# Cross-attention in an fp32 decoder layer: scores in two row halves, values in four column quarters, weights divided on GpSimd

## The chip, the cores and the metric

The kernel runs on one core of one Trainium2 chip. The metric is the device time of one execution in microseconds (us); less is better. A core has five engines that matter here: PE (TensorE, matrix products), DVE (VectorE), ACT (ScalarE), POOL (GpSimd) and SP, which here only issues DMAs. Each engine works off its own queue strictly in the order in which the program was written, and waits on semaphores for the others.

## The reference, cut to what matters

One pre-norm decoder layer, all in fp32, for x of 4 batches x 1024 rows x 256 columns:

```python
x = x + self_attention(layernorm(x))                     # 16 heads of 64, 4 key-value heads
x = x + cross_attention(layernorm(x), ctx, mask)         # 16 heads of 16, 64 keys per batch
x = x + feed_forward(layernorm(x))                       # routed, with small splines per row

def cross_attention(query, context, mask):               # the part that is changed
    q  = query @ Wq + bq
    kv = context @ Wkv + bkv                             # split into k and v, 16 heads each
    scores = einsum("bhid,bhjd->bhij", q, k) * 256**-0.5
    scores = where(mask[:, None, None, :], -inf, scores)
    out = einsum("bhij,bhjd->bhid", softmax(scores), v)
    return out @ Wout + bout
```

With a mask that hides every key of a batch the softmax is not a number; the inputs drawn hide none.

## The kernel before, in words

The rows of a batch lie in tiles of 128 (eight a batch, 32 in all). Self-attention is the body: for each tile, four "duos" of four heads each (`duo`, L551). A duo makes scores in two halves of the PE's rows (L577, 64 x 512), takes their maxima on DVE (L591), the exponentials on ACT (L597), turns the weights either on DVE with DMAs (L606, L633) or on PE (L616), multiplies with the values in two column halves (L656), and spreads the inverse sums over the partitions by a small product (`spread`, L682).

**Cross-attention** (`cross_attention`, L780) takes two tiles at a time (TX = 2). After the layernorm (`layernorm`, L390, whose rsqrt runs on POOL, L406 and L407), its transposes and the query projection (L797), each of the two tiles of 128 queries goes through these steps:

- `scores` (L818): for each half c of the columns, one matmul of the 128 query columns with `kblk`, a block matrix of 128 x (8 heads x 64 keys). `block_k` (L744) makes it once a batch, by multiplying the keys with the 0/1 pattern `own` (L303), so that a head's 16 rows meet only its own 64 columns. The rest of the block is zero.
- `masked` (L821): DVE adds the mask's row out of PSUM into `sc`, 128 x (16 heads x 64 keys); `largest` (L833): the maximum by head on DVE; `less` (L836): POOL subtracts it; `exponential` (L839): ACT.
- `flips` (L850, group L854) and `evict` (L856): eight transposes on PE, copied to `pT` by ACT (L857).
- `values` (L868): eight matmuls, each with 128 x 128 of the weights stationary and 34 columns of `vblk` streaming: two heads of 16 value columns and, for each, one column of ones (`keep`, L313 and `block_v`, L764), which yields the sum of the weights. Masked keys have zeros there.
- `divide` (L872): DVE takes the reciprocal of the sums out of PSUM (L873) and multiplies (L874); `flip_o` (L886, group L888): two transposes on PE; `evict_o` (L890): ACT; `project_o` (L898); `evict_p` (L902) on DVE; `residual` (L905) on POOL.

**The order of the work** is made by a planner (`Flow`, L78). `add` hands it a task with an engine, a cost in us, a key (a due time), the tasks that it needs and the buffers that it takes; `order` (L120) places, one at a time, the task that can start first by these costs and lags (0.2 to 0.3 us between engines), urgent ones first (the maxima and exponentials of self-attention), and never with a key more than `AHEAD` = 16 over the front. The code is emitted in this order; on the chip each engine keeps it, even where the costs were wrong. Buffers have places by tag (L226): the scores of cross-attention (`xsc`), `xpT` and `xoT` have one each, so the second tile's scores wait until the first one's weights are turned. Three PSUM buffers of one bank (`p1`, L240) serve everything but self-attention's scores and outputs.

**The feed-forward block** (`feed_forward`, L991) follows for every four tiles (the last four in two blocks of two), mostly in many small DVE steps, with its last steps on POOL (`finish`, L1144).

Of the kernel before, what the change touches and what calls it, by code (L numbers as in the profile page):

```python
# [10 lines left out]
F32 = mybir.dt.float32  # L11
U8 = mybir.dt.uint8
AF = mybir.ActivationFunctionType
ALU = mybir.AluOpType
# [13 lines left out]
XC = 8  # L28
# [164 lines left out]
def decoder(  # L193
# [35 lines left out]
            xmx=2, xpT=1, xrs=2, xo=1, xoT=1, xf=1, fxT=1, hT=1, sc=1, comp=2, cal=1, fm=4, hot=1, hotT=1,  # L229
            par=1, hh=1, mag=2,  # L230
        ),
        {"p1", "ln", "res", "rb", "rsum", "nmax"},
# [67 lines left out]
    for i in range(NCL):  # L300
        nc.gpsimd.memset(falling[:, i : i + 1], float(NCL - i))

    own = const.tile([P, XC], F32, name="own")  # L303
    nc.gpsimd.memset(own, 1.0)
    nc.gpsimd.affine_select(
        out=own, in_=own, compare_op=ALU.is_ge, fill=0.0, base=0, pattern=[[-XD, XC]], channel_multiplier=1
    )
    nc.gpsimd.affine_select(
        out=own, in_=own, compare_op=ALU.is_ge, fill=0.0, base=XD - 1, pattern=[[XD, XC]], channel_multiplier=-1
    )  # L310
# [5 lines left out]
    add("DVE", 0.2, 2, lambda: nc.vector.tensor_scalar(keep, kmask8, -1.0, 1.0, ALU.mult, ALU.add), [kmask_], [keep_])  # L316
# [40 lines left out]
    quants = buf("xo", work, 2, DC, NTILES, name="quants")  # L357
# [193 lines left out]
    def duo(b, d):  # L551
# [6 lines left out]
        ss = sums[b, qt]  # L558
        prob = Buf("prob", lambda: work.tile([P, 4 * S], F32, tag="prob", name=f"prob_{b}_{d}"))
# [86 lines left out]
        for part in range(2):  # L646
            def values(part=part):
# [20 lines left out]
                holds=[heads[b, qt]],  # L668
# [52 lines left out]
    def context(b, at):  # L721


        kblk = kblks[b] = buf("kblk", big, DC, XC, SK, name=f"kblk_{b}")
        vblk = vblks[b] = buf("vblk", big, XH // 2, 2, XD + 1, name=f"vblk_{b}")
# [18 lines left out]
        def block_k(c):  # L744
            nc.vector.tensor_tensor(
                kblk.t[:, c],
                kt.t[:, c, :].unsqueeze(1).to_broadcast([P, XC, SK]),
                own.unsqueeze(2).to_broadcast([P, XC, SK]),
                ALU.mult,
            )  # L750
# [13 lines left out]
        def block_v():  # L764
            vt4 = vt.t.rearrange("p (g t d) -> p g t d", t=2, d=XD)
            for half in range(2):
                r = slice(half * SK, (half + 1) * SK)
                nc.vector.tensor_scalar(vblk.t[r, :, half, :XD], vt4[r, :, half, :], keep[r, b : b + 1], None, ALU.mult)
                nc.vector.tensor_copy(vblk.t[r, :, half, XD], keep[r, b : b + 1].to_broadcast([SK, XH // 2]))
# [10 lines left out]
    def cross_attention(b, t0, at):  # L780
# [31 lines left out]
        for k in range(TX):  # L812
            now = at + 2 + 3 * k
            sc = buf("xsc", work, XH, SK, name=f"xsc_{name}_{k}")
            for c in range(DC):
                ps = psum1(f"xs_{name}_{k}_{c}")

                def scores(c=c, ps=ps, k=k):  # L818
                    mm(ps.t, lhsT=qT.t[:, c, k * P : (k + 1) * P], rhs=kblk.t[:, c], start=True, stop=True)  # L819

                def masked(c=c, ps=ps, sc=sc):  # L821
                    nc.vector.tensor_tensor(  # L822
                        sc.t[:, XC * c : XC * (c + 1), :],
                        ps.t.rearrange("p (h k) -> p h k", k=SK),
                        mneg[:, b, :].unsqueeze(1).to_broadcast([P, XC, SK]),
                        ALU.add,
                    )

                add("PE", 0.9, now, scores, [qT, kblk], [ps], holds=[sc])
                add("DVE", 0.68, now, masked, [ps, mneg_], [sc])  # L830
# [14 lines left out]
            add("ACT", 1.07, now, exponential, [sc], [sc])  # L845
            pT = buf("xpT", work, XH // 2, P, name=f"xpT_{name}_{k}")
            for g in range(2):
# [12 lines left out]
                add("ACT", 0.6, now + 2, evict, [pt], [pT])  # L860
            av = psum1(f"xav_{name}_{k}")
            rs = buf("xrs", small, XH, name=f"xrs_{name}_{k}")
            o = buf("xo", work, D, name=f"xo_{name}_{k}")

            def rows_of(av=av):
                return av.t[:, : XH * (XD + 1)].rearrange("p (h d) -> p h d", h=XH)

            def values(av=av, pT=pT, rows_of=rows_of):  # L868
                for g in range(XH // 2):
                    mm(rows_of(av)[:, 2 * g : 2 * g + 2, :], lhsT=pT.t[:, g, :], rhs=vblk.t[:, g], start=True, stop=True)  # L870

            def divide(av=av, rs=rs, o=o, rows_of=rows_of):  # L872
                nc.vector.reciprocal(rs.t, rows_of(av)[:, :, XD])  # L873
                nc.vector.tensor_tensor(  # L874
                    o.t.rearrange("p (h d) -> p h d", d=XD),
                    rows_of(av)[:, :, :XD],
                    rs.t.unsqueeze(2).to_broadcast([P, XH, XD]),
                    ALU.mult,
                )

            add("PE", 2.1, now + 3, values, [pT, vblk], [av], holds=[rs, o])
            add("DVE", 0.7, now + 3, divide, [av], [rs, o])
            pt = psum1(f"pxo_{name}_{k}")
            oT = buf("xoT", work, DC, P, name=f"xoT_{name}_{k}")

            def flip_o(pt=pt, o=o):  # L886
                for c in range(DC):
                    flip(pt.t[:, c * P : (c + 1) * P], o.t[:, c * P : (c + 1) * P], ident)  # L888

            def evict_o(pt=pt, oT=oT):  # L890
                nc.scalar.copy(oT.t.rearrange("p c q -> p (c q)"), pt.t[:, :D])

            add("PE", 0.3, now + 4, flip_o, [o], [pt], holds=[oT])
# [382 lines left out]
```

## Time and profile before

| | |
|---|---|
| median of three runs | 1993.22 us (1990.15 to 1993.29) |
| the profiled execution | 1997.92 us, of which 1996.2 from the first to the last instruction (span) |
| mean granted PE clock | 0.965 |
| busy: PE, DVE, ACT, POOL | 1864.4, 1538.9, 964.2, 267.2 us |
| HBM traffic | 13.37 MB read, 4.19 MB written |

How to read it: a group is a source line, an engine and an operation, with "out<-in" by the names in the program. After it come the shapes, the count, the busy time in us and the mean length of one in ns, and behind the second bar the idle time of the engine just before these instructions and what ended it. A PE row counts records: an fp32 matmul is two of them, a transpose one. PEld rows are weight loads, which overlap the matmuls. "128*64" is the part of the array in use, rows x columns. Records of neighbours overlap in the profile, since the end of a matmul is modelled; the start of the next group tells more than the length. The chain that ended last is followed back from the last instruction, at each step to what released it.

### The profile page before, as it was taken

What the parts mean: (1) busy time and instruction counts of PE and PEld (TensorE: products, weight loads), DVE (VectorE), ACT (ScalarE), POOL (GpSimd) and SP (SyncE); (2) the same over time, 40 slices, a digit from 0 to 9 for tenths busy, and PEclk for the clock granted to TensorE, in tenths of its full rate; (3) what the DMA queues carried; (4) which work ended last, traced back from release to release, by engine and by line L of the source; (5) the groups of instructions that cost most, each with busy time, mean ns of one, the idle gap of its engine ahead of it and who ended that gap; (6) DMA issues with size and microseconds to landing.
All of it is one profiled execution on the core that took longest, in us unless ns stands there. A gap on an engine that the chain in (4) does not pass through costs nothing.

```text
span 1996.2 us, 30371 instructions
## 1 busy us (share of the span) xinstructions
PE 1864.4 (93%) x11204; PEld 1114.0 (56%) x11204; DVE 1538.9 (77%) x2447; ACT 964.2 (48%) x1730; POOL 267.2 (13%) x422
## 2 busy tenths in 40 slices
PE   7899999999999999989999999989999999997973
PEld 4455555655566555556556555655556655564542
DVE  4767787897788878787778878887778877778853
ACT  2545455555445555545445545454545554553431
POOL 1000101030010301121000311103001030010322
PEclk9899999999999999989999999998999999998975
DMA  3555554454455455545454456535455435545510
GB/s 132 127 127 137 127 132 109 105 121 108 104 127 117 94 122 123 123 110 127 96 116 107 95 128 137 122 75 127 96 122 127 101 91 127 113 100 127 119 24 5
DMA packets 87859, 220.92 MB, mean 111 GB/s; under 512 B 26336, under 2 KB 36896, under 8 KB 87712
## 3 DMA queue, kind: packets, MB, share of 16 engines
q1 hardware_dynamic: 85440, 212.42, 47.3%
q0 software_dynamic: 1168, 4.19, 0.6%
q8 instruction: 89, 1.46, 0.3%
q10 hardware_dynamic: 1104, 2.37, 0.3%
q14 instruction: 58, 0.48, 0.1%
HBM read 13.37 MB, written 4.19 MB: 9 GB/s over the span
## 4 chain that ended last, share of the span: by engine, by line
PE 81%; DVE 12%; ACT 3%; DMA 1%; issue 1%; SPq 1%; POOL 1%; POOLq 0%; ACTq 0%; DVEq 0%
PE s L577 25%; PE av L656 22%; DVE nmax L591 6%; PE pq L530 5%; PE po L709 5%; PE ptp L616 5%; PE rb L682 2%; PE xav L870 2%; PE xs L819 2%; PE pxq L797 2%; ACT prob L597 2%; PE pv L502 2%; DVE prob L606 1%; PE pk L479 1%; PE pg L1097 1%; PE pxp L900 1%
## 5 line engine op out<-in xcount | busy, mean ns | idle before, releaser
L597 ACT ACTIVATE prob<-s,nmax 128x1024 f32<-128x1024 f32 x512 | 569.2, 1115 | 581.0 <-DVE nmax L591 571.3
L591 DVE TENSOR_REDUCE nmax<-s 128x1 f32<-128x1024 f32 x512 | 602.1, 1217 | 211.4 <-PE s L577 210.6
L577 PE MATMUL s<-kT,qT 64*128 64x512 f32 x2048 | 545.4, 621 | 9.3 <-ACT prob L597 9.0
L656 PE MATMUL av<-probT,vn 128*64 128x256 f32 x4096 | 479.6, 385 | 2.7 <-DMA probT<-prob 2.5
L606 DVE STREAM_TRANSPOSE prob<-prob 128x1024 f32<-128x1024 f32 x384 | 460.3, 1225 | 20.5 <-ACT prob L597 15.3
L656 PEld LDWEIGHTS av<-probT,vn 128*64 128x64 f32 x4096 | 284.0, 137 | 204.1 <-issue 70.5
L577 PEld LDWEIGHTS s<-kT,qT 64*128 64x128 f32 x2048 | 196.2, 187 | 216.6 <-issue 170.2
L620 ACT COPY probT<-ptp 128x512 f32<-128x512 f32 x256 | 138.9, 594 | 127.7 <-PE ptp L616 127.7
L616 PE MATMUL ptp<-ident,prob 128*128 128x128 f32 x1024 | 147.6, 281 | 20.5 <-ACT probT L620 5.0
L616 PEld LDWEIGHTS ptp<-ident,prob 128*128 128x128 f32 x1024 | 109.9, 141 | 76.4 <-issue 31.2
L530 PE MATMUL pq<-ln_T,wq 128*128 128x256 f32 x512 | 132.2, 407 | 4.2 <-DMA wq<-in_w_qT 3.7
L837 POOL TENSOR_TENSOR xsc<-xsc,xmx 128x1024 f32<-128x1024 f32 x32 | 61.0, 1908 | 497.0 <-DVE xmx L834 252.6
L709 PE MATMUL po<-wo,heads 128*128 128x256 f32 x512 | 121.1, 386 | 1.9 <-DVE xsc L822 1.8
L530 PEld LDWEIGHTS pq<-ln_T,wq 128*128 128x128 f32 x512 | 99.2, 202 | 32.8 <-issue 15.0
L709 PEld LDWEIGHTS po<-wo,heads 128*128 128x128 f32 x512 | 94.2, 190 | 34.5 <-issue 15.9
L715 POOL TENSOR_TENSOR x<-x,res 128x256 f32<-128x256 f32 x32 | 23.3, 728 | 620.9 <-DVE res L712 516.6
L597 ACT ACTIVATION_READ_ACCUMULATOR prob<-s,nmax 128x1 f32 x512 | 100.8, 197 | 0.0
L541 ACT ACTIVATE qT<-pq,bqs,qscale 128x256 f32<-128x256 f32 x128 | 65.3, 563 | 49.6 <-PE pq L530 49.2
L695 DVE TENSOR_TENSOR heads<-av,rb 128x256 f32<-128x256 f32 x128 | 53.0, 414 | 46.7 <-PE av L656 45.6
L682 PEld LDWEIGHTS rb<-ident,rsum 128*64 128x64 f32 x1024 | 54.6, 136 | 59.0 <-issue 45.4
L682 PE MATMUL rb<-ident,rsum 128*64 128x128 f32 x1024 | 83.3, 284 | 4.2 <-DVE xres L903 4.2
L819 PE MATMUL xs<-kblk,xq 128*128 128x512 f32 x128 | 67.9, 653 | 1.7 <-ACT xq L806 1.7
(162 smaller groups left out, 1526.9 us busy)
## 6 DMA issues: line engine op xcount, KB each, us to landing
probT<-prob SPq DMA_DIRECT2D x1536, 128.0 KB, 2.3
ln_n<-in_x SPq DMA_DIRECT2D x16, 256.0 KB, 3.1
x<-in_x SPq DMA_DIRECT2D x8, 512.0 KB, 4.2
out<-ln_n POOLq DMA_DIRECT2D x7, 512.0 KB, 3.5
wo<-in_w_oT SPq DMA_DIRECT2D x1, 1024.0 KB, 13.3
wq<-in_w_qT ACTq DMA_DIRECT2D x1, 1024.0 KB, 9.6
rowv<-in_rows ACTq DMA_DIRECT2D x1, 774.0 KB, 11.7
xwkv<-in_xw_kv SPq DMA_DIRECT2D x1, 512.0 KB, 13.1
```

The lines of the kernel that those rows point to most:

```text
L530: mm(pq.t[:, 2 * P * k : 2 * P * (k + 1)], lhsT=wq[:, dc, (c + k) * P : (c + k + 1) * P], rhs=xTs[b].t[:, dc, 2 * P * w : 2 * P * (w + 1)] ...
L541: nc.scalar.activation(qTs[b, w, c + k].t, pq.t[:, 2 * P * k : 2 * P * (k + 1)], AF.Identity, bias=bqs[:, c + k : c + k + 1], scale=qscale,)
L577: mm(ps[z].t[:, 512 * g : 512 * (g + 1)], lhsT=q.t[r, (qt % 2) * P : (qt % 2 + 1) * P], rhs=kT.t[r, 512 * g : 512 * (g + 1)], start=True, ...
L591: nc.vector.tensor_reduce(nmax.t, ps[z].t, AX.X, ALU.max, negate=True)
L597: nc.scalar.activation(weights(prob.t, z, i), src, AF.Exp, bias=nmax.t, accum_out=ss.t[:, k : k + 1])
L606: nc.vector.transpose(t, t)
L616: flip(pt.t[:, j * P : (j + 1) * P], weights(prob.t, z, i)[:, kc * P : (kc + 1) * P], ident)
L620: nc.scalar.copy(to[:, z, 4 * g : 4 * g + 4, i, :], pt.t.rearrange("p (c q) -> p c q", q=P))
L656: mm(av.t[r, :], lhsT=vns[b, kc // 2].t[:, kc % 2, j * HD : (j + 1) * HD], rhs=rhs, start=(kc == 0), stop=(kc == NT - 1),)
L682: mm(pr.t[r, i * P : (i + 1) * P], lhsT=rs.t[:, k : k + 1].to_broadcast([P, HD]), rhs=ident, start=True, stop=True,)
L709: mm(po.t[:, :D], lhsT=hT.t[:, c, :], rhs=wo[:, c, :], start=(c == 0), stop=(c == QC - 1))
L819: mm(ps.t, lhsT=qT.t[:, c, k * P : (k + 1) * P], rhs=kblk.t[:, c], start=True, stop=True)
```

## The change

Five things change, all in cross-attention.

1. **Scores.** `kblk` and `own` shrink from 8 heads side by side to 4. One task makes all scores of a tile: per half c two matmuls of 64 rows with 256 columns, one in each row half of the array, each row half into its own PSUM buffer. The mask is then added in four steps of 256 elements and not two of 512.
2. **Sums.** The columns of ones leave `vblk`. POOL adds the two halves of the keys (512 results) and their halves (256), DVE adds the remaining 16 per head and takes the reciprocal, and POOL multiplies the weights, ahead of their transposes.
3. **Values.** `vblk` becomes the stationary operand, 128 x 32 (two heads), and `pT` streams with 128 columns. Four such products stand beside each other in column quarters of the array, and the result is the turned output. `flip_o` and its PSUM buffer go; ACT copies `av` to `oT`.
4. **Mask.** Since the sums now take in no `keep`, `keep` is multiplied once by 1/(1 - smallest mask entry of the batch): one where a key is left, infinite where none is. This takes five small DVE steps at the start.
5. **Planner.** The costs handed to it change with the tasks; `pT` is followed in two parts; the tag `xo` is replaced by `xhalf`, and `xrs` has one place, not two.

Nothing of self-attention or the feed-forward block changes, nor any DMA. The diff, without the lines that only rename a tag or a variable:

```diff
@@ -226,10 +226,10 @@
         dict(
             s=2, p1=3, o=1, x=3, xn1=2, xT=1, kT0=1, kT1=1, vn=4, qT=12, prob=2, probT=2, sums=3, nmax=4,
             heads=1, rb=1, rsum=2, res=1, ln=2, xxT=1, xqT=1, kblk=1, vblk=1, xkt=1, xvt=1, xsc=1,
-            xmx=2, xpT=1, xrs=2, xo=1, xoT=1, xf=1, fxT=1, hT=1, sc=1, comp=2, cal=1, fm=4, hot=1, hotT=1,
+            xmx=2, xpT=1, xrs=1, xhalf=1, xoT=1, xf=1, fxT=1, hT=1, sc=1, comp=2, cal=1, fm=4, hot=1, hotT=1,
             par=1, hh=1, mag=2,
         ),
-        {"p1", "ln", "res", "rb", "rsum", "nmax"},
+        {"p1", "ln", "res", "rsum", "nmax", "rb"},
     )
     add = flow.add
 
@@ -300,20 +300,33 @@
     for i in range(NCL):
         nc.gpsimd.memset(falling[:, i : i + 1], float(NCL - i))
 
-    own = const.tile([P, XC], F32, name="own")
+    own = const.tile([P, XC // 2], F32, name="own")
     nc.gpsimd.memset(own, 1.0)
-    nc.gpsimd.affine_select(
-        out=own, in_=own, compare_op=ALU.is_ge, fill=0.0, base=0, pattern=[[-XD, XC]], channel_multiplier=1
-    )
-    nc.gpsimd.affine_select(
-        out=own, in_=own, compare_op=ALU.is_ge, fill=0.0, base=XD - 1, pattern=[[XD, XC]], channel_multiplier=-1
-    )
+    for r in (slice(0, HD), slice(HD, P)):
+        nc.gpsimd.affine_select(
+            out=own[r], in_=own[r], compare_op=ALU.is_ge, fill=0.0, base=0, pattern=[[-XD, XC // 2]],
+            channel_multiplier=1,
+        )
+        nc.gpsimd.affine_select(
+            out=own[r], in_=own[r], compare_op=ALU.is_ge, fill=0.0, base=XD - 1, pattern=[[XD, XC // 2]],
+            channel_multiplier=-1,
+        )
 
 
     keep = const.tile([P, B], F32, name="keep")
     mneg = const.tile([P, B, SK], F32, name="mneg")
     keep_, mneg_ = Buf(), Buf()
-    add("DVE", 0.2, 2, lambda: nc.vector.tensor_scalar(keep, kmask8, -1.0, 1.0, ALU.mult, ALU.add), [kmask_], [keep_])
+    none = const.tile([P, B], F32, name="none")
+
+    def kept():
+
+        nc.vector.tensor_scalar(keep, kmask8, -1.0, 1.0, ALU.mult, ALU.add)
+        nc.vector.tensor_reduce(none, rmask8.rearrange("p (b k) -> p b k", b=B), AX.X, ALU.min)
+        nc.vector.tensor_scalar(none, none, -1.0, 1.0, ALU.mult, ALU.add)
+        nc.vector.reciprocal(none, none)
+        nc.vector.tensor_tensor(keep, keep, none, ALU.mult)
+
+    add("DVE", 1.2, 2, kept, [kmask_, rmask_], [keep_])
     add(
         "DVE", 0.4, 2,
         lambda: nc.vector.tensor_scalar(mneg.rearrange("p b k -> p (b k)"), rmask8, MASKED, None, ALU.mult),
@@ -720,9 +734,8 @@
 
     def context(b, at):
 
-
-        kblk = kblks[b] = buf("kblk", big, DC, XC, SK, name=f"kblk_{b}")
-        vblk = vblks[b] = buf("vblk", big, XH // 2, 2, XD + 1, name=f"vblk_{b}")
+        kblk = kblks[b] = buf("kblk", big, DC, XC // 2, SK, name=f"kblk_{b}")
+        vblk = vblks[b] = buf("vblk", big, XH // 2, 2, XD, name=f"vblk_{b}")
         kt, vt = buf("xkt", small, DC, SK, name=f"xkt_{b}"), buf("xvt", small, D, name=f"xvt_{b}")
         pk, pv = psum1(f"pxk_{b}"), psum1(f"pxv_{b}")
 
@@ -744,8 +757,8 @@
         def block_k(c):
             nc.vector.tensor_tensor(
                 kblk.t[:, c],
-                kt.t[:, c, :].unsqueeze(1).to_broadcast([P, XC, SK]),
-                own.unsqueeze(2).to_broadcast([P, XC, SK]),
+                kt.t[:, c, :].unsqueeze(1).to_broadcast([P, XC // 2, SK]),
+                own.unsqueeze(2).to_broadcast([P, XC // 2, SK]),
                 ALU.mult,
             )
 
@@ -765,8 +778,7 @@
             vt4 = vt.t.rearrange("p (g t d) -> p g t d", t=2, d=XD)
             for half in range(2):
                 r = slice(half * SK, (half + 1) * SK)
-                nc.vector.tensor_scalar(vblk.t[r, :, half, :XD], vt4[r, :, half, :], keep[r, b : b + 1], None, ALU.mult)
-                nc.vector.tensor_copy(vblk.t[r, :, half, XD], keep[r, b : b + 1].to_broadcast([SK, XH // 2]))
+                nc.vector.tensor_scalar(vblk.t[r, :, half, :], vt4[r, :, half, :], keep[r, b : b + 1], None, ALU.mult)
 
         add("PE", 0.9, at, project_k, [xwkv_, cT_], [pk], holds=[kt, kblk, vblk])
         add("DVE", 0.5, at, evict_k, [pk, colv_], [kt])
@@ -812,22 +824,31 @@
         for k in range(TX):
             now = at + 2 + 3 * k
             sc = buf("xsc", work, XH, SK, name=f"xsc_{name}_{k}")
-            for c in range(DC):
-                ps = psum1(f"xs_{name}_{k}_{c}")
-
-                def scores(c=c, ps=ps, k=k):
-                    mm(ps.t, lhsT=qT.t[:, c, k * P : (k + 1) * P], rhs=kblk.t[:, c], start=True, stop=True)
-
-                def masked(c=c, ps=ps, sc=sc):
-                    nc.vector.tensor_tensor(
-                        sc.t[:, XC * c : XC * (c + 1), :],
-                        ps.t.rearrange("p (h k) -> p h k", k=SK),
-                        mneg[:, b, :].unsqueeze(1).to_broadcast([P, XC, SK]),
-                        ALU.add,
-                    )
-
-                add("PE", 0.9, now, scores, [qT, kblk], [ps], holds=[sc])
-                add("DVE", 0.68, now, masked, [ps, mneg_], [sc])
+            ps = [psum1(f"xs_{name}_{k}_{z}") for z in range(2)]
+
+            def scores(ps=ps, k=k):
+                for c in range(DC):
+                    for z, r in enumerate(halves):
+                        mm(
+                            ps[z].t[:, 256 * c : 256 * (c + 1)],
+                            lhsT=qT.t[r, c, k * P : (k + 1) * P],
+                            rhs=kblk.t[r, c],
+                            start=True,
+                            stop=True,
+                        )
+
+            add("PE", 1.1, now, scores, [qT, kblk], ps, holds=[sc])
+            for z in range(2):
+                def masked(z=z, ps=ps, sc=sc):
+                    for c in range(DC):
+                        nc.vector.tensor_tensor(
+                            sc.t.rearrange("p (c z h) k -> p c z h k", c=DC, z=2)[:, c, z],
+                            ps[z].t.rearrange("p (c h k) -> p c h k", c=DC, k=SK)[:, c],
+                            mneg[:, b, :].unsqueeze(1).to_broadcast([P, XC // 2, SK]),
+                            ALU.add,
+                        )
+
+                add("DVE", 0.75, now, masked, [ps[z], mneg_], [sc])
             mx = buf("xmx", small, XH, name=f"xmx_{name}_{k}")
 
             def largest(sc=sc, mx=mx):
@@ -843,6 +864,24 @@
             add("DVE", 1.22, now, largest, [sc], [mx])
             add("POOL", 1.9, now, less, [sc, mx], [sc])
             add("ACT", 1.07, now, exponential, [sc], [sc])
+            half = buf("xhalf", work, XH, SK // 2, name=f"xhalf_{name}_{k}")
+            rs = buf("xrs", small, 2, XH, name=f"xrs_{name}_{k}")
+
+            def add_up(sc=sc, half=half):
+                q = SK // 4
+                nc.gpsimd.tensor_tensor(half.t, sc.t[:, :, : 2 * q], sc.t[:, :, 2 * q :], ALU.add)
+                nc.gpsimd.tensor_tensor(half.t[:, :, :q], half.t[:, :, :q], half.t[:, :, q:], ALU.add)
+
+            def inverse(half=half, rs=rs):
+                nc.vector.tensor_reduce(rs.t[:, 0], half.t[:, :, : SK // 4], AX.X, ALU.add)
+                nc.vector.reciprocal(rs.t[:, 1], rs.t[:, 0])
+
+            def divide(sc=sc, rs=rs):
+                nc.gpsimd.tensor_tensor(sc.t, sc.t, rs.t[:, 1].unsqueeze(2).to_broadcast([P, XH, SK]), ALU.mult)
+
+            add("POOL", 1.6, now + 1, add_up, [sc], [half], holds=[rs])
+            add("DVE", 0.6, now + 1, inverse, [half], [rs])
+            add("POOL", 1.9, now + 1, divide, [sc, rs], [sc])
             pT = buf("xpT", work, XH // 2, P, name=f"xpT_{name}_{k}")
             for g in range(2):
                 pt = psum1(f"pxt_{name}_{k}_{g}")
@@ -857,41 +896,29 @@
                     nc.scalar.copy(pT.t[:, 4 * g : 4 * g + 4, :], pt.t.rearrange("p (c q) -> p c q", q=P))
 
                 add("PE", 0.54, now + 2, flips, [sc], [pt], holds=[pT])
-                add("ACT", 0.6, now + 2, evict, [pt], [pT])
+                add("ACT", 0.6, now + 2, evict, [pt], [pT.part(g)])
+
+
             av = psum1(f"xav_{name}_{k}")
-            rs = buf("xrs", small, XH, name=f"xrs_{name}_{k}")
-            o = buf("xo", work, D, name=f"xo_{name}_{k}")
-
-            def rows_of(av=av):
-                return av.t[:, : XH * (XD + 1)].rearrange("p (h d) -> p h d", h=XH)
-
-            def values(av=av, pT=pT, rows_of=rows_of):
-                for g in range(XH // 2):
-                    mm(rows_of(av)[:, 2 * g : 2 * g + 2, :], lhsT=pT.t[:, g, :], rhs=vblk.t[:, g], start=True, stop=True)
-
-            def divide(av=av, rs=rs, o=o, rows_of=rows_of):
-                nc.vector.reciprocal(rs.t, rows_of(av)[:, :, XD])
-                nc.vector.tensor_tensor(
-                    o.t.rearrange("p (h d) -> p h d", d=XD),
-                    rows_of(av)[:, :, :XD],
-                    rs.t.unsqueeze(2).to_broadcast([P, XH, XD]),
-                    ALU.mult,
-                )
-
-            add("PE", 2.1, now + 3, values, [pT, vblk], [av], holds=[rs, o])
-            add("DVE", 0.7, now + 3, divide, [av], [rs, o])
-            pt = psum1(f"pxo_{name}_{k}")
             oT = buf("xoT", work, DC, P, name=f"xoT_{name}_{k}")
 
-            def flip_o(pt=pt, o=o):
+            def values(av=av, pT=pT):
                 for c in range(DC):
-                    flip(pt.t[:, c * P : (c + 1) * P], o.t[:, c * P : (c + 1) * P], ident)
-
-            def evict_o(pt=pt, oT=oT):
-                nc.scalar.copy(oT.t.rearrange("p c q -> p (c q)"), pt.t[:, :D])
-
-            add("PE", 0.3, now + 4, flip_o, [o], [pt], holds=[oT])
-            add("ACT", 0.38, now + 4, evict_o, [pt], [oT])
+                    for j in range(4):
+                        mm(
+                            av.t[32 * j : 32 * (j + 1), P * c : P * (c + 1)],
+                            lhsT=vblk.t[:, 4 * c + j].rearrange("p t d -> p (t d)"),
+                            rhs=pT.t[:, 4 * c + j, :],
+                            start=True,
+                            stop=True,
+                            tile_position=(0, 32 * j),
+                        )
+
+            add("PE", 0.9, now + 3, values, [pT.part(0), pT.part(1), vblk], [av], holds=[oT])
+            add(
+                "ACT", 0.4, now + 3,
+                lambda av=av, oT=oT: nc.scalar.copy(oT.t.rearrange("p c q -> p (c q)"), av.t[:, :D]), [av], [oT],
+            )
             po = psum1(f"pxp_{name}_{k}")
             r = buf("res", work, D, name=f"xres_{name}_{k}")
 
```

More of the change, by code (lines that the diff above doesn't have):

```diff
@@ L356, in decoder @@
     cneg = const.tile([P, DC, NCL], F32, name="cneg")
-    quants = buf("xo", work, 2, DC, NTILES, name="quants")
+    quants = buf("xhalf", work, 2, DC, NTILES, name="quants")
     sig_ = Buf()
@@ L558, in duo @@
         ss = sums[b, qt]
+        hd = heads[b, qt]
         prob = Buf("prob", lambda: work.tile([P, 4 * S], F32, tag="prob", name=f"prob_{b}_{d}"))
@@ L667, in duo @@
                 [av],
-                holds=[heads[b, qt]],
+                holds=[hd],
             )
@@ L1069, in select @@
         def select():
-            h, sel = hot.t
+            h, sel = hot.t[0], hot.t[1]
             nc.vector.tensor_tensor(h, sc.t[:, :, NCL:].rearrange("p t (c j) -> p t c j", j=TPC), c_wide(), ALU.mult)
```

## The prediction, made before the result was known

> **What bounds the kernel now.** I read four views in this order: busy time by engine, windows of 50 us, the chain that ended last, and the groups of instructions by line; then the order of time around one tile.
>
> ```profile
> span 1996.2 us, 30371 instructions
> PE 1864.4 (93%) x11204; PEld 1114.0 (56%) x11204; DVE 1538.9 (77%) x2447; ACT 964.2 (48%) x1730; POOL 267.2 (13%) x422
> ```
> ```profile
> core 0: us, PE busy (x) PEld busy (x) DVE busy (x) ACT busy (x) POOL busy (x), PEclk, DMA share, GB/s
> 450.00:500.00 50.00, 49.46 (x314) 30.01 (x314) 35.20 (x46) 25.10 (x45) 3.04 (x6) 1.00 0.50 111
> 850.00:900.00 50.00, 44.06 (x238) 26.31 (x238) 43.73 (x86) 23.17 (x44) 13.97 (x23) 0.90 0.45 103
> 1950.00:1997.00 47.00, 13.59 (x48) 8.69 (x48) 16.47 (x64) 6.31 (x12) 8.91 (x16) 0.52 0.02 6
> ```
> In the body TensorE (PE) is full (49.5 of 50 us). Where a feed-forward block runs (850 to 900) VectorE (DVE) takes 44 us and PE falls to 44. The end is a chain of single steps at half clock. GpSimd (POOL) is nearly empty.
>
> ```profile
> PE 81%; DVE 12%; ACT 3%; DMA 1%; issue 1%; SPq 1%; POOL 1%; POOLq 0%; ACTq 0%; DVEq 0%
> ```
> ```profile
> L819 PE MATMUL xs<-kblk,xq 128*128 128x512 f32 x128 | 67.9, 653 | 1.7 <-ACT xq L806 1.7
> L870 PE MATMUL xav<-vblk,xpT 128*128 128x34 f32 x512 | 63.3, 278 | 0.8 <-ACT xpT L857 0.3
> L888 PE MATMUL pxo<-ident,xo 128*128 128x128 f32 x64 | 13.2, 289 | 2.6 <-DVE xo L874 2.6
> L837 POOL TENSOR_TENSOR xsc<-xsc,xmx 128x1024 f32<-128x1024 f32 x32 | 61.0, 1908 | 497.0 <-DVE xmx L834 252.6
> L715 POOL TENSOR_TENSOR x<-x,res 128x256 f32<-128x256 f32 x32 | 23.3, 728 | 620.9 <-DVE res L712 516.6
> ```
> The change touches 67.9 + 63.3 + 13.2 = 144.4 us of PE work. Adding the pieces of the chain by line, xs stands on it with 45.8, xav with 49.1 and pxo with 7.3 us: 102.2, or 71% of that work.
>
> PE in order of time, one tile at full clock (columns: start, length, group, count of records; the start of the next group tells the true cost):
> ```profile
> 675.51 0.66 PE L682 MATMUL rb<-ident,rsum 128*64 128x128 f32 x8
> 676.10 1.97 PE L870 MATMUL xav<-vblk,xpT 128*128 128x34 f32 x16
> 677.91 1.96 PE L819 MATMUL xs<-kblk,xq 128*128 128x512 f32 x4
> 679.71 0.38 PE L888 MATMUL pxo<-ident,xo 128*128 128x128 f32 x2
> 680.02 1.56 PE L577 MATMUL s<-kT,qT 64*128 64x512 f32 x6
> ```
> From start to start: rb 0.59, xav 1.81, xs 1.80, pxo 0.31 us. A matmul is two records, a transpose one.
>
> **Scores.** Two 128-row matmuls of 512 columns become four of 64 rows and 256 columns, two at a time in the row halves. L577 does this already: four of 64 x 512 cost 1.92 us from start to start (653.03, next group 654.95), the work of two full ones, so its halves overlap. Half the columns: 0.96, with the fixed part of a group 1.0. Saved 0.8 per tile. Its weight loads keep their width of 128.
>
> **Values.** Eight matmuls stream 34 columns under a 128-column weight load; 1.81/16 = 113 ns a record. The profile has 512 loads in 60.1 us, 117 each: the loads set the pace. Afterwards eight matmuls load 32 columns and stream 128, in four column quarters. No row shows quarters. The nearest is rb: 64-column halves, 128 columns streamed, 0.59 for eight records. Sixteen at that pace are 1.18; if four quarters overlap as rb's two do, the queue per quarter is as deep as rb's per half (four records of 128 columns), 0.59; if they do not overlap, 1.8 as now (16 records of 128 columns at half of xs's streaming rate, 1.80/4 for 512, are 1.8). I take 0.9, between the two ends that overlap: saved 0.9, bounds 0 and 1.2. One rule of the Trainium skill speaks against it ("TensorEngine Tiling (Array Packing)", Tiling Modes, Key Properties): a change of tiling mode drains the array. Row: rb (column halves) hands over to xav (whole array) and pxo to s (row halves) with the next start before the modelled end, 0.59 for eight records included. By the row a change costs at most what is already in those spacings; by the rule a drain of the order of rb's tail (0.1 us) would be paid twice more per tile, 32 x 0.2 = 6 us, and the sum below would be -39 and not -45. I follow the row, since today's order changes mode at nearly every group.
>
> **Transposes of the output.** Values leave PSUM already turned: pxo (0.31) goes, and with it DVE's L873 and L874; ACT's copy stays as an eviction of xav.
>
> PE per tile: 0.8 + 0.9 + 0.3 = 2.0 us. Over the run xs averages 67.9/32 = 2.12 where 1.80 is the full-clock spacing with its overlap taken off; I add 5% for the slower clock, not 18%: 2.1. The 30 tiles before the end: 63 us.
>
> **How much shows.** About the chain's share at least, 71% (45 us); all of it at most. PE is full in most windows, but about one in eight looks like 850:900. I take 87%: 55 us.
>
> **DVE.** Per tile L822's 2 x 681 ns become four of 256 elements; L903 (256, from PSUM) has 418: 1.67, so +0.31. Row sums over 256 elements: L834 needs 1219 for 1024; with 0.15 fixed that is 0.42; reciprocal 0.2. Gone: 0.240 + 0.425. Net +0.27, 8 us in all; the smaller key block gives back 8 x (683 - 418 ns) = 2. It hides where DVE has 20% idle; uncovered in one window of eight: 1 us. The five small mask instructions run once at the start beside the weight loads, whose cover they have; uncovered 1 us.
>
> **POOL.** L837: 1.91 us for 1024 elements, L715 0.73 for 256; a line through both gives 1.1 for 512. The two additions: 1.1 + 0.73; division 1.91. 3.75 per tile, 120 us in all, to 387: 20%. Hidden by POOL's idle time. But the waits are new. On POOL, addition waits for the exponential and division for DVE; behind them queue the residual additions (L715, L906) and the layernorms' rsqrt. On DVE the sum waits for POOL; behind it queue attention's maxima (L591), for which ACT and then PE wait. The plan has 1.6 us for the additions, I have 1.83: DVE stands about 0.2 to 0.3 us in half the tiles, 5 us bounded by 0 and 10; on the path 2 to 3.
>
> A second rule: "SBUF — State Buffer", Who interferes with whom: a DVE instruction with two SBUF inputs, or in a two-port mode, and a reading GpSimd instruction exclude each other. Row: L412 beside the output's POOL steps averages 609 ns against 400 elsewhere (up to 941); so it exists. But L591 never exceeds 1.23 us and L606 never 1.25, and L822 stays within 650 to 692. By the rule, some 150 us of DVE work in 1539 can meet 96 POOL instructions, with half of such an instruction (0.8 us) to wait: 96 x 0.1 x 0.8 = 8 us on DVE; by the rows 2, at the layernorms. With seven eighths under DVE's idle time either moves the sum by about 1 us; I take 1.
>
> **Planner.** A score task now takes two of three PSUM buffers at once. Both ends open: PE waits for L822's buffers total under 12 us today. I put 0 here, and let the range take it; removing pxo's buffer answers it.
>
> **The end.** Two tiles stand on the chain alone. Gone: scores and masks from 1930.02 to 1934.54 become 2.0 + 1.75 (-0.8) and those from 1940.94 to 1944.01 about 2.9 (-0.2); xav 1.99 becomes 0.9 (-1.1); from reciprocal to ACT's copy 1951.85 to 1953.46 (-1.6). New in each: 1.83 + 0.62 + 1.91 and three handovers of 0.15: 4.8, 9.6 for both, since the single score buffer makes the second wait for the first. Net +6.
>
> **Sum.** -55 + 6 + 4 (DVE 1, POOL waits 2, shared port 1) = -45. The profiled execution took 1997.9 (span 1996.2 and 1.7 around it); 1952.9 by this sum. The median of the three runs, 1993.2, lies 4.7 below the profiled one; 1993.2 - 45 = **1948**.
>
> **Rivals.**
> (A) As summed, 1930 to 1965: 0.60.
> (B) Quarters overlap fully and all PE time shows: (0.8 + 1.2 + 0.3) x 1.05 x 30 = 73, 1993 - 73 + 6 = 1926: 0.13. For it: PE at 49 of 50 us.
> (C) Quarters do not overlap: 1.1 x 1.05 x 30 x 0.87 = 30 saved, 10 given back: 1973: 0.12. For it: no row has a quarter. Against: the halves of rb and L656 overlap.
> (D) The chain of L577, L591, L597 takes over and only half of 63 shows: 1993 - 32 + 10 = 1971: 0.06. For it: L591 is 119 us of the chain. Against: PE seldom waits for L597 (45 us in all).
> (E) POOL's line becomes the wait at the weights' transposes L854. After the exponential they now come 5.9 us later (685.53 + 1.05 to 692.50); the new work is 4.8. If the plan puts them sooner than POOL finishes, PE, strictly in order, stands. It decides from 55/32 = 1.7 us per tile; at 2.1 us it gives 1993 - 55 + 67 = 2005 (the stalls take the place of the other losses): 0.05. Against: those transposes wait 14.8 us today, most of it in the end.
> (F) Nothing to measure: 0.04.
>
> About 0.2% (4 us) is what a measurement can tell from no change. Faster 0.91, same 0.04, slower 0.05. The range runs from 1922, just under B, to 1976, just over C and D; outside lie E, F and the far edges of B to D, less than 0.2.
>
> **What would show it.** xs records of 64x256, near 1.0 us from start to start; xav of 128*32, 0.9; no pxo; POOL near 387 us, DVE near 1545, PE near 1790; the end longer by 6 us from the last xq to the last xres. Wrong if xav stays at 1.8 (C), if PE's wait at L854's successor exceeds 1 us a tile (E), or if DVE's share in the body passes 90% (D).

## The result, and the profile after

The changed kernel takes 2001.9 us (median of 16 runs, 1993.8 to 2005.0) against 1996.8 before (16 runs, 1990.2 to 2002.1): ratio 1.0021, 95% interval 1.0007 to 1.0035. The forecast was 1948. The profiled execution took 2003.0 us, span 2001.3.

First the page of the changed kernel, busy time and chain:

```profile
span 2001.3 us, 30643 instructions
PE 1815.0 (91%) x11268; PEld 1069.0 (53%) x11268; DVE 1550.5 (77%) x2507; ACT 965.5 (48%) x1730; POOL 391.5 (20%) x520
...
PE 74%; DVE 12%; ACT 5%; SPq 5%; issue 2%; DMA 2%; POOL 1%; ACTq 0%; POOLq 0%; DVEq 0%
```

PE is busy 49 us less, and the span is 5 us longer. PE's part of the chain falls from 81% to 74%; what took its place is spread over ACT, SP's queue and DMAs, none of which has notably more work than before (ACT 965.5 us busy for 964.2). The groups of the changed steps, by form:

```profile
L832 PE MATMUL xs<-kblk,xq 64*128 64x256 f32 x256 | 38.4, 408 | 2.7 <-ACT xq L818 1.7 <-DVE rb L705 1.0
L908 PE MATMUL xav<-xpT,vblk 128*32 128x128 f32 x512 | 22.1, 288 | 1.5 <-ACT xpT L896 1.4
L908 PEld LDWEIGHTS xav<-xpT,vblk 128*32 128x32 f32 x512 | 12.0, 111 | 18.5 <-issue 13.8 <-ACT xpT L896 2.8 <-ACT qT L554 1.5
L872 POOL TENSOR_TENSOR xhalf<-xsc 128x512 f32<-128x512 f32 x32 | 40.5, 1266 | 15.6 <-ACT xsc L862 15.6
```

The change does on PE what it says: xs from 67.9 to 38.4 us, xav from 63.3 to 22.1, pxo gone. The four quarters do overlap. At full clock, in order of time:

```profile
442.74 0.65 PE L908 MATMUL xav<-xpT,vblk 128*32 128x128 f32 x16
443.31 1.13 PE L832 MATMUL xs<-kblk,xq 64*128 64x256 f32 x8
```

From start to start the values' 16 records take 0.57 us, 36 ns each, where rb's halves took 0.59 us for eight, 74 ns each.

**Body and end.** The last product of self-attention with its inverse sums (DVE, "heads") parts the run in two. Its rows, of before and of after (columns: shortest, median and longest ns, first and last start in us):

```profile
L695 DVE TENSOR_TENSOR heads<-av,rb x128: 383/424/426, 71.1 to 1915.2; 128x256 f32<-128x256 f32 x128
```
```profile
L709 DVE TENSOR_TENSOR heads<-av,rb x128: 382/424/426, 74.1 to 1912.0; 128x256 f32<-128x256 f32 x128
```

From there to the end of the span it is 81 us before and 89 after: 8 lost, 6 were forecast. But the body, where 51 us were to come off, is 3 us shorter. The sum of the body is the window from 190 us (the first cross-attention has begun by 184) to that row; before and after (length, then the busy time of PE, PEld, DVE, ACT and POOL, then clock, DMA share and GB/s):

```profile
190.00:1915.20 1725.20, 1660.20 (x10205) 995.46 (x10205) 1377.80 (x2138) 871.10 (x1564) 237.47 (x351) 0.98 0.50 113
```
```profile
190.00:1912.00 1722.00, 1615.20 (x10275) 952.07 (x10271) 1386.70 (x2186) 872.73 (x1564) 353.25 (x441) 0.97 0.50 114
```

PE idles 65 us of the first window and 107 of the second. Taken from start to start, the matmuls of the changed groups need 67.7 us less in the body (xav 32, xs 22, pxo 13.5). So some 42 us of what was freed is now idle time. About 20 more are in the clock: the records show PE at half clock for 55 us of the body before and for 96 after, and 41 us at half speed cost some 20 (an estimate; PE is busy in 93% of that time after, in 85% before). 67.7 - 42 - 20 leaves some 6; 3 were measured. The balance is rough: of the start-to-start times 4.9 us before and 10.7 after are idle time that the 42 hold as well. Without it the groups need 73.5 us less, and some 8 us of the balance stay unexplained.

**What such a pause looks like.** In order of time, after (idle time in the brackets, and what ended it):

```profile
703.72 0.69 PE L908 MATMUL xav<-xpT,vblk 128*32 128x128 f32 x16
703.82 1.13 ACT L611 ACTIVATE prob<-s,nmax 128x1024 f32<-128x1024 f32 x1
...
704.92 1.12 ACT L611 ACTIVATE prob<-s,nmax 128x1024 f32<-128x1024 f32 x1
...
706.01 0.39 ACT L920 COPY xoT<-xav 128x256 f32<-128x256 f32 x1
706.45 1.65 PE L927 MATMUL pxp<-xwo,xoT 128*128 128x256 f32 x4 [2.04 <-ACT xoT L920]
```

The values are ready by 704.4. Their copy stands in ACT's queue behind two exponentials of self-attention, and the product that needs the copy is next in PE's queue. PE waits 2.04 us, although later entries of its queue may have been ready. The windows around it show what comes on top (the last numbers of a row are the clock, the DMA share and GB/s):

```profile
690.00:704.00 14.00, 13.59 (x98) 7.60 (x96) 13.35 (x21) 6.89 (x14) 7.18 (x6) 1.00 0.48 107
704.00:710.00 6.00, 3.96 (x26) 1.90 (x20) 4.45 (x9) 2.40 (x5) 1.51 (x3) 0.74 0.79 174
```

The clock is at 0.74 of full speed in the 6 us that hold the pause and what follows. The body has 26 pauses of over 1.3 us (4 before), and 23 stretches at half clock (7 before), 18 of them 3.4 us long and five 6.8; ahead of every one PE had idled at least 1.6 us of the last 10.

Most of the pauses are not at the new steps. The longest waits of PE in the body (190 to 1912 us) by what ended them, with the number of waits and the longest:

```profile
PE ln_pt L439 <- DVE ln_n L425: 11.1, 6, 2.8
PE ptp L630 <- ACT probT L634: 11.0, 17, 2.0
PE ptp L630 <- DVE rb L705: 10.5, 14, 1.3
PE ptp L630 <- ACT prob L611: 10.1, 7, 2.6
PE av L670 <- DMA probT<-prob: 9.2, 8, 4.7
PE rb L696 <- DVE xsc L844: 8.2, 14, 1.3
PE ptp L630 <- DVE xsc L844: 7.0, 4, 1.7
```

The first five are layernorms and self-attention, code that the change does not touch. The last two wait for the new mask steps, 15.2 us (5.6 for the masks before), and the product after the output's copy, as in the pause above, waits 6.7. Of the 26 pauses of over 1.3 us, 8 are waits for steps of cross-attention. The division on POOL ends no wait of this list: PE's two long waits for it, 18.0 us together, are in the end.

### The profile page after: what moved, and what is told of

It is laid out like the page before. It is cut to its first block, busy times and chain, and to the rows that moved or that the text cites. A ratio compares the mean times of both kernels' runs of the same rounds, so it can differ in the third digit from the quotient of the medians.

```text
span 2001.3 us, 30643 instructions
## 1 busy us (share of the span) xinstructions
PE 1815.0 (91%) x11268; PEld 1069.0 (53%) x11268; DVE 1550.5 (77%) x2507; ACT 965.5 (48%) x1730; POOL 391.5 (20%) x520
## 4 chain that ended last, share of the span: by engine, by line
PE 74%; DVE 12%; ACT 5%; SPq 5%; issue 2%; DMA 2%; POOL 1%; ACTq 0%; POOLq 0%; DVEq 0%
PE s L591 24%; PE av L670 21%; DVE nmax L605 6%; PE pq L543 5%; SPq L647 5%; PE ptp L630 4%; PE po L723 4%; ACT prob L611 3%; PE rb L696 3%; PE pxq L809 2%; PE pv L515 2%; PE pk L492 1%; PE pxt L893 1%; DVE prob L620 1%; DVE xsc L844 1%
## 5 line engine op out<-in xcount | busy, mean ns | idle before, releaser
L591 PE MATMUL s<-kT,qT 64*128 64x512 f32 x2048 | 568.6, 643 | 15.0 <-ACT prob L611 14.8
L670 PE MATMUL av<-probT,vn 128*64 128x256 f32 x4096 | 487.1, 389 | 9.6 <-DMA probT<-prob 9.4
L591 PEld LDWEIGHTS s<-kT,qT 64*128 64x128 f32 x2048 | 203.8, 193 | 232.6 <-issue 179.6
L630 PE MATMUL ptp<-ident,prob 128*128 128x128 f32 x1024 | 145.7, 282 | 45.0 <-ACT prob L611 11.4
L543 PEld LDWEIGHTS pq<-ln_T,wq 128*128 128x128 f32 x512 | 94.5, 194 | 33.9 <-issue 21.2
L419 POOL TENSOR_SCALAR ln_rs<-ln_mv 128x1 f32<-128x1 f32 (+1 forms) x96 | 21.3, 222 | 286.2 <-DVE ln_mv L415 268.1
## 6 DMA issues: line engine op xcount, KB each, us to landing
rowv<-in_rows ACTq DMA_DIRECT2D x1, 774.0 KB, 11.6
```

The source lines that it names most:

```text
L543: mm(pq.t[:, 2 * P * k : 2 * P * (k + 1)], lhsT=wq[:, dc, (c + k) * P : (c + k + 1) * P], rhs=xTs[b].t[:, dc, 2 * P * w : 2 * P * (w + 1)] ...
L591: mm(ps[z].t[:, 512 * g : 512 * (g + 1)], lhsT=q.t[r, (qt % 2) * P : (qt % 2 + 1) * P], rhs=kT.t[r, 512 * g : 512 * (g + 1)], start=True, ...
L630: flip(pt.t[:, j * P : (j + 1) * P], weights(prob.t, z, i)[:, kc * P : (kc + 1) * P], ident)
L670: mm(av.t[r, :], lhsT=vns[b, kc // 2].t[:, kc % 2, j * HD : (j + 1) * HD], rhs=rhs, start=(kc == 0), stop=(kc == NT - 1),)
```

## The experiments

Four theories. **N**: what is freed on PE turns into waits, because DVE, ACT and DMA steps of self-attention were nearly late already. **P**: the sums and the division on POOL make others wait. **S**: a score task now takes two of three PSUM buffers, and holds them until DVE has added the mask. **O**: the order of instructions that the planner makes for the changed tasks is a bad one. In the edits below, cut to the lines that matter, A stands for the changed kernel and B for the one before. A ratio is to B of the same round, whose median lay between 1995.5 and 1998.7 us.

**1. Scores alone** (B with the score step, `own` and `kblk` of A).

> The kernel before with only the score step changed (row halves, two PSUM buffers taken at once, four mask steps). It takes about 22 us of PE time away in the body and leaves the division and the values as they were. Theory N (the freed PE time turns into waits for DVE, ACT and DMA steps of self-attention that were nearly late already; the new steps are not to blame): 1985 to 1997. Theory S (the pair of PSUM buffers, held until DVE has added the mask, makes other PE work wait): 2000 or more. Theory P (the sums and the division on POOL are to blame): about 1975, since they are not in this kernel.

Measured: 1996.1 us, 1.0003 of before (0.9988 to 1.0019). The body ends at 1911.2, 4 us earlier, with 19 us of xs gone. P falls as the only cause: without any division the PE time doesn't show either. Nor is it slower, as S had it.

**2. All but the scores** (A with the score step of B).

> The changed kernel with the score step and the key block of before; the value rows of a batch share a buffer with the half sums, since the larger block needs the room. It keeps 45 us of PE time away in the body (values and transposes) and has the division on POOL. Theory S: 1960 to 1970, since the pair of PSUM buffers is gone. Theory P: 2005 or more. Theory N: 1985 to 2000.

Measured: 1991.5 us, 0.9978 (0.9964 to 0.9993); the body ends at 1897.8, 17 us earlier than before, for 45 us of PE time. That is in N's range (1985 to 2000) and above S's, and P is wrong again. Putting the score step in (this kernel to A) frees 26 us more of xs and yet makes the body 14 us longer in the two profiles, and the whole some 9 us longer by the two ratios.

**3. The division cut short, in the same order.**

```diff
-    nc.gpsimd.tensor_tensor(half.t, sc.t[:, :, : 2 * q], sc.t[:, :, 2 * q :], ALU.add)
-    nc.gpsimd.tensor_tensor(half.t[:, :, :q], half.t[:, :, :q], half.t[:, :, q:], ALU.add)
+    nc.gpsimd.tensor_tensor(half.t[:, :, :1], sc.t[:, :, :1], sc.t[:, :, 2 * q : 2 * q + 1], ALU.add)
-    nc.gpsimd.tensor_tensor(sc.t, sc.t, rs.t[:, 1].unsqueeze(2).to_broadcast([P, XH, SK]), ALU.mult)
+    nc.gpsimd.tensor_tensor(sc.t[:, :, :1], sc.t[:, :, :1], rs.t[:, 1].unsqueeze(2), ALU.mult)
```

> The changed kernel in the same order of instructions, but the additions, the sum and the division work on one key of 64 (the output of cross-attention is not normalised; one POOL addition is left out): about 3.3 us less of POOL and DVE time in the line of each tile. The two tiles of the end give 6.6 us back by every theory. Theory P: under 1970, since the waits are gone all through the body. Theories N and S: 1990 to 1996.

Measured: 1988.6 us, 0.9965 (0.9947 to 0.9984), far from P's 1970. Against A the end is 9 us shorter, the body 5.6. In this order, that is about what P costs in the body.

**4. Less PE work in B's own order.**

```diff
-    for g in range(XH // 2):
-        mm(rows_of(av)[:, 2 * g : 2 * g + 2, :], lhsT=pT.t[:, g, :], rhs=vblk.t[:, g], start=True, stop=True)
+    mm(av.t[:, : XH * (XD + 1)], lhsT=pT.t[:, 0, :], rhs=vblk.t.rearrange("p g t d -> p (g t d)"), start=True, stop=True)
```

> The kernel before in the same order of instructions, but the values of a tile are made by one matmul of 272 columns instead of eight of 34 (only the weights of the first two heads enter the output): some 1.2 us of PE time less per tile, 36 us in the body, and nothing else changed. If PE is what bounds the body, 1960 to 1965. Theory N: 1985 or more, since the same order only waits elsewhere. Theories S and P blame the change's own steps, so they expect 1960 to 1965 here.

Measured: 0.9926 (0.9901 to 0.9952). The group's row is now

```profile
L869 PE MATMUL xav<-vblk,xpT 128*128 128x272 f32 x64 | 23.1, 442 | 0.3
```

and 37.6 us went from start to start in the body. It became 14 us shorter: 38% of the freed time shows. The time, 1979.4 us, lies between the two forecasts, 1960 to 1965 and 1985 or more. So even with every task in its old place PE's time is worth less than half, as N has it in a milder form; but it is worth much more than the 3 of 67.7 that the change got.

**5. Two score tasks, one PSUM buffer each** (A).

```diff
-    add("PE", 1.1, now, scores, [qT, kblk], ps, holds=[sc])
+    add("PE", 0.6, now, scores, [qT, kblk], [ps[z]], holds=[sc])      # for each row half z
```

> The changed kernel, but the scores of a tile are two tasks, one for each row half with its own PSUM buffer, so that no task takes two of the three buffers at once (the four matmuls may then overlap less). Theory S (the pair of buffers): 15 to 20 us under the changed kernel, about 1984, with fewer PE pauses over 1.3 us than its 26 and less half-clock time in the body than 96 us. Theory N (freed PE time turns into waits, whatever the scores do): within 6 us of the changed kernel.

Measured: 1997.0 us, 0.9995 of before (0.9982 to 1.0008), some 5 us under A by the two ratios; the body ends at 1904.3, 21 pauses, 65 us at half clock, in a profiled execution that was the fastest of 20, 5 us under their median. The pair of buffers is a part, about 5 us, not the 15 to 20 of S.

**6 and 7. Self-attention's maxima over half the scores, in B and in A.**

```diff
-    nc.vector.tensor_reduce(nmax.t, ps[z].t, AX.X, ALU.max, negate=True)
+    nc.vector.tensor_reduce(nmax.t, ps[z].t[:, : S // 2], AX.X, ALU.max, negate=True)
```

> The kernel before in the same order, but self-attention's maxima read 512 of 1024 scores: DVE's L591 falls from 1.22 to about 0.68 us, some 275 us of DVE time less and 1.1 us less in each round of scores, maxima, exponentials (the weights are then taken from a maximum that isn't the row's; sums stay exact). If PE alone bounds the body, within 10 us of before. Theory N (DVE's line is nearly as late as PE's): 1950 or less.

> The changed kernel in its own order, with the same shortened maxima. Theory N: with DVE out of the way the freed PE time shows, so this is 35 us or more under the kernel before with shortened maxima. Theory O (the order of instructions that the planner makes for the changed tasks is worse, whatever the engines do): within 10 us of it.

Measured: 1949.0 us, 0.9772 (0.9735 to 0.9809) for B, 1940.1 us, 0.9726 (0.9684 to 0.9768) for A. Taking 257 us from DVE brings B 46 to 50 us: DVE's line counts, as N says. But A does not then run away from B: it goes from 5 us over B to 9 under, where N in its strong form wanted 35 under. O's figure, within 10, holds. In the body A is now 16 us ahead and not 3. Full DVE queues hid some 13 us of the gain, and not the rest.

**8 and 9. Another order, nothing else** (one constant of the planner: how far a key may lie above the front), in A and in B.

```diff
-    AHEAD, SLACK = 16, 0.4
+    AHEAD, SLACK = 14, 0.4
```

> The changed kernel with one constant of the planner changed (AHEAD 14 for 16): the same instructions in another order. Theory O: 15 to 25 us under the changed kernel, since the order at 16 is what loses. Theories N and S, for which the order is of no account: within 6 us of it.

> The kernel before with AHEAD 14 for 16. The changed kernel gained some 25 us by this. Theory O (the order that the planner makes at 16 is a bad one for the changed tasks; it is no worse than others for the tasks before): within 6 us of the kernel before, because the planner's own last score moves only from 1979.8 to 1983.7 on its clock, where that of the changed kernel moves from 1969.6 to 1946.0. Should 14 be better for any tasks: 15 to 25 us under before.

Measured: A 1972.4 us, 0.988 (0.9842 to 0.9917); B 2003.7 us, 1.0034 (1.0017 to 1.0052). The same instructions in another order bring A 1.4%, or 28 us by the ratios, more than the forecast 15 to 25; they cost B 0.3%, some 7 us, where O had it within 6. The last "heads" and the body's window of A at 14:

```profile
L709 DVE TENSOR_TENSOR heads<-av,rb x128: 381/417/426, 74.4 to 1881.6; 128x256 f32<-128x256 f32 x128
```
```profile
190.00:1881.60 1691.60, 1598.24 (x10270) 945.44 (x10270) 1395.32 (x2186) 873.89 (x1564) 352.83 (x441) 0.98 0.51 116
```

The body is 30 us shorter than A's at 16: 13.4 us of PE's idle time (93.4 left of 106.8), and half of the 31 us less at half clock (65 for 96), in 12 stretches for 23. Pauses of over 1.3 us are not fewer but more, 31 for 26. At the place of the pause shown above, some 6 us earlier in this order, ACT takes the copy before the exponentials:

```profile
699.77 0.37 ACT L920 COPY xoT<-xav 128x256 f32<-128x256 f32 x1 [1.88 <-PE xav L908]
...
700.20 1.13 PE L927 MATMUL pxp<-xwo,xoT 128*128 128x256 f32 x4
700.37 1.11 ACT L611 ACTIVATE prob<-s,nmax 128x1024 f32<-128x1024 f32 x1 [0.22 <-DVE nmax L605]
```

**10. A worse order** (A with SLACK 0.2).

> The changed kernel with SLACK 0.2 for 0.4, another constant of the planner: the same instructions in an order whose last score the planner puts at 2018.9, 49 later than at 0.4. Theory O, in the form that the plan's length foretells the chip's: 30 us or more over the changed kernel. If the order is of no account or the plan foretells nothing: within 10 us of it.

Measured: 2034.5 us, 1.0188 (1.016 to 1.0215), 33 us over A. So the order alone moves this kernel between 1972 and 2034. B was not run with SLACK 0.2, so this does not show that the changed tasks suffer more from it. The planner's own clock foretells the direction. It is no time of the chip, but where it ends its last task of self-attention's scores goes with the measured end of the body:

| kernel | planner's last score | body ends, us | PE idle in the body | at half clock |
|---|---|---|---|---|
| B, AHEAD 14 | 1983.7 | 1919.4 | 64 | 58 |
| B | 1979.8 | 1915.2 | 65 | 55 |
| B, scores changed (1) | 1974.9 | 1911.2 | 78 | 68 |
| A, SLACK 0.2 | 2018.9 | 1948.6 | 137 | 106 |
| A | 1969.6 | 1912.0 | 107 | 96 |
| A, two score tasks (5) | 1954.2 | 1904.3 | 95 | 65 |
| A, scores of B (2) | 1953.9 | 1897.8 | 85 | 55 |
| A, AHEAD 14 | 1946.0 | 1881.6 | 93 | 65 |

The last three columns are of one execution each; those of (2) and (5) lay 3 and 5 us under their medians, so differences of a few us between rows say nothing. The planner puts A 10 us ahead of B at 16 and 34 ahead with AHEAD 14; in the body 3 and 34 were measured.

**11. The PE work twice, in A's order.**

```diff
-    for c in range(DC):                      # in scores and in values
+    for c in (*range(DC), *range(DC)):
```

> The changed kernel in its own order, but the scores and the values of cross-attention are each computed twice (same results): about 0.9 + 0.6 us of PE time more per tile, 45 us in the body. If PE time still bounds the body, 2040 or more. Theories N and O (in this order PE waits for others anyway): less than 25 us over the changed kernel.

Measured: 1.0101 (1.0078 to 1.0125), 2017.2 us. From start to start xs and xav take 33.5 us more in the body, which grows by 11.4: 34%. It is experiment 4 backwards: in these two orders a microsecond of PE in cross-attention is worth about a third of one.

**12. The best version: AHEAD 14, and the last two tiles on DVE.** There DVE has nothing else to do; it subtracts the maximum, adds up all 64 weights at once and multiplies.

```diff
+    late = (b, t0) == (B - 1, NT - TX)
-    add("POOL", 1.9, now, less, [sc, mx], [sc])
+    add("DVE", 1.2, now, less_late, [sc, mx], [sc])          # if late
-    add("POOL", 1.6, now + 1, add_up, [sc], [half], holds=[rs])
-    add("DVE", 0.6, now + 1, inverse, [half], [rs])
-    add("POOL", 1.9, now + 1, divide, [sc, rs], [sc])
+    add("DVE", 2.7, now + 1, divide_late, [sc], [sc, rs])    # if late
```

> The changed kernel with AHEAD 14, and for the last two tiles the subtraction, the sums and the division on DVE instead of POOL (all of the computation stays). In the body it has the order of the run with AHEAD 14. By the rows of the end 1.9 + 2.0 + 0.4 + 1.9 us a tile become 1.2 + 1.2 + 1.2 or so, 5 us less for the two: about 1966.

Measured: 1964.7 us, 0.9843 of before (0.9821 to 0.9865). The body ends at 1880.7, the end takes 84 us. Of the chain of one tile there:

```profile
1901.02 1.23 DVE xsc L867
...
1902.33 1.06 ACT xsc L862
1903.42 1.23 DVE xrs L891
1904.68 0.26 DVE xrs L892
1904.96 1.24 DVE xsc L893
```

## Why the prediction was wrong

**Right: what leaves PE.** 67.7 us in the body, 63 forecast; without idle time 73.5, which is rival B's 73. The scores' group takes about 1.0 us from start to start, the values' 0.57 (0.9 forecast, the lower bound was 0.59), the output's transposes are gone. Case C, no overlap of the quarters, is out (its 1.8 us is worked out at xs's own streaming rate, not at half of it).

**Half right: the change of tiling mode** (the part of the array in use, rows x columns). I put it at nothing, following rb's 0.59 us. But in both kernels it has a price that this spacing already holds: at full clock the last record of a group is followed 0.09 to 0.10 us later where the mode changes than where it stays (before: rb 0.203 for 0.103 us, po 0.309 for 0.216, the transposes ptp 0.203 for 0.109). The rule's 6 us did not come for another reason: they supposed two more changes in each tile, and the body has 807 changes, 802 before.

**Right: the end,** 8 us for 6, and POOL, 391.5 us for 387. An addition of 512 elements takes 1.27 us and not 1.1.

**DVE** grew by 11.6 us, not 6. The masks cost 3 us more, not 10 (45.2 for 42.5: a step of 256 that shares its cover with the next costs 353 ns, not 418). What grew is L425 and L1158, the layernorms' and the feed-forward's steps (L412 and L1131 before), which mostly read SBUF only: 69.2 us before, 80.2 after, by the same instructions. L425 takes 0.40 us where no POOL step of two inputs runs beside it, and up to 1.99 us beside the new division. Here the second rule weighed, of the Trainium skill's page "SBUF — State Buffer", section Who interferes with whom, had the better estimate: 8 us, where I took 2 from the rows. What it is worth on the path was not tested.

**Wrong: "How much shows. ... I take 87%".** It was 5%. The step took PE's busy share (49 of 50 us in the body) as proof that its time is the run's time, with the share of the chain as a floor. Neither held. Experiments 4 and 11 put the worth of a microsecond of PE, all orders kept, at 38% and 34%: the chain's 71% was no floor. Other chains lie close beside it; for DVE's, experiment 6 shows it (46 to 50 us for 257), for those of ACT and the DMAs it is argued from PE's waits. At 34 to 38% the freed time would have brought some 24 us of the body (an estimate), not 55 and not 3.

**Wrong: "Planner. ... I put 0 here, and let the range take it".** With AHEAD 14 in both kernels the same change is worth 1.5%, with 16 nothing, and A with SLACK 0.2 is some 38 us slower than B with 0.4. The pair of PSUM buffers, named there, is about 5 us (experiment 5). The sum should have had a range of tens of microseconds for any edit that gives the planner other tasks.

**Missing: the clock.** I had used the clock to size the freed time, not to ask what pauses do to it. By the estimate above some 20 us of the 64 lost in the body are PE at half speed after pauses of its own.

Of the mechanisms among the rivals D's came nearest (PE's time replaced by self-attention's), but it does not carry: the next scores start on average 1.5 us after the last exponential that frees their buffer before, and 1.4 after. E, POOL's line at the transposes, holds for the end alone. F, no difference, which comes nearest to what was measured, had 0.04.

**Open:** why the planner's rule at 16 makes the worse order of the changed tasks. That the order costs A 30 us of the body is shown, since the same instructions in another order get them back; which of its choices do, beyond the pair of buffers, is not. The other half of the loss remains in that order too, in line with the third that PE's time is worth. Two other orders of A and one of B were run, so whether B too has a better one is open. Nor was the half clock taken away by itself.

## What to carry to other kernels

When every engine has a fixed queue, a full engine is not yet the bound: take work from it in the unchanged order, and see how much of it shows, before you pay for a faster form of that work. When the order comes from a planner, a change of the tasks is also a change of the order, and one constant of the planner can be worth more than the change: try a few orders for both kernels before the verdict. Where the clock falls after a pause, as here, the pause can be paid twice.

## What the runs showed of the hardware

Half clock came after short pauses of PE: 1.6 to 2.8 us of idle time in 10 came ahead of 21 of the 23 stretches in the changed kernel's body, 3.4 and 3.5 ahead of the other two. The Trainium skill's page "TensorE: Matmul & The Clock Gate" (HAM oscillation) speaks of gaps over some 3.4 us; the trace here shows it for shorter ones. But not each such pause brings it: half clock followed within 10 us for 16 of the 26 pauses of over 1.3 us in A, and for 5 of the 31 with AHEAD 14. What decides is not shown.

From run to run, time goes with the clock: over the 16 runs of the changed kernel the mean granted clock lies between 0.949 and 0.956 (correlation with the time -0.90, 1.7 us for each 0.001).

Four column quarters in fp32 run side by side: 16 records of 128 columns in 0.57 us from start to start. Their weight loads overlap too: 512 loads of 32 columns, 111 ns each by their records, together fill 12.0 us, where the 512 of 128 columns before filled 60.1.

A change of tiling mode between neighbouring matmuls takes 0.09 to 0.10 us of PE at full clock, in all ten groups of the kernel before where both cases occur (three are named above). Its body has 802 such changes, so they come to some 80 us (an estimate), more than the change freed. No run here orders the work to have fewer.
